# Third level's weights split over VectorE and GpSimd, and the mixed kernels one step later in a round

## The chip, the cores and the metric

The kernel runs on one core of a Trainium2 chip. The metric is the device time of one execution in microseconds (us). PE is the TensorE matmul engine, PEld its weight loads, DVE is VectorE, ACT is ScalarE, POOL is GpSimd and SP is the engine that issues most DMAs.

## The reference

Two blocks are added to a residual stream `x` of 32 x 128 x 2048 in fp32. The first block is a conditioned 1x1 convolution (a mixture of eight 128 x 128 kernels for each batch entry), followed by a dense layer of 2048 x 2048 whose weight has sixteen low-rank updates. The second is a grouped convolution of nine taps followed by a per-head feed-forward part. The change lies in the dense layer:

```python
out = jnp.einsum('bsd,od->bso', x, W) + bias
xa = jnp.einsum('bsd,erd->ebsr', x, A)
w = coeffs * scales
upd = jnp.einsum('ebsr,eor,e->bso', xa, Bf, w)
return out + upd
```

In the kernel the mixture is applied after the dense layer, so that the dense product takes `x` itself, and the low-rank updates are folded into `W`.

## The kernel before, in words

**The dense product** is a matrix product by recursion of the kind that replaces eight block products by seven (each with sums and differences of blocks as operands). The outermost level gives seven **rounds**, `ROUNDS = ("P1", "P2", "P6", "P7", "P5", "P3", "P4")`. A round has eight **steps** `g` = 0 to 7, one for each group of four batch entries. Inside a step the second level gives seven products again, named P1 to P7 too; each is four chained fp32 matmuls of 128 x 128 by 128 x 512 into a PSUM bank, which DVE then adds into an SBUF accumulator.

**The third level** is applied to one of these seven, in the rounds of `THIRD` (all but P1 and P4, with pair 3 left out in three of them). There two neighbouring steps, `g` even and `g` odd, form a **pair**. `multiply_third` runs only five of the seven products in each step (P1, P5, P6, P3, P7), and what P2 and P4 would have done for both steps is done in the odd step by seven **quarters**: each is four matmuls of 128 x 128 by 128 x 256, and their order among the products is P1, *P1q*, *P2q*, P5, *P6q*, *P5q*, P6, *P7q*, *P3q*, P3, *P4q*, P7. The operands of the quarters are
- the third level's **weights** `quarters`: sums and differences of the halves of the round's P2 weights (tile `_q0`) and P4 weights (tile `_q1`), made once in a round by `third_weights` (lines 387 to 390, in the profile `P_q`). For each of the two tiles and two values of `kc` there are four operations on 128 x 256, sixteen in all;
- the third level's **inputs** `sq`, made for each pair by `third_inputs` (lines 406 to 409): four operations on 128 x 512.

Quarters P1q and P2q read neither; P6q is the first to read both, `t[:, 1]` of each.

**The order of the work** is written out by hand: under `manual_schedule` each engine runs its instructions in program order. In step `i` of the main loop POOL first combines the next step's inputs (`x_combine`: line 282 for sums of x blocks and lines 310 to 313 for `s_P`), then makes `sq` if `g` is even (in round P6 DVE does so after the step), at `g` = 7 makes the second level's weights of the next round (`inner_weights`, lines 252 to 256, tiles `P_t`; its `t4` holds the P4 weights), and at `g` = 0 runs `third_weights`. The call `inner_weights` of step 7 comes after the `x_combine` for the next round's step 0; then follow, at `g` = 0, the `x_combine` for step 1, `sq` and `third_weights`. SP issues the loads in program order too: accumulators for the next step (`olds_load`, line 272) and x for the step after (`x_loads`, line 267). All these tiles come from one pool of 24 slots of 1 MB, and a tile waits for the release of the slot that it gets.

**Between the products** of a step `between(j)` puts small work on DVE. `mixed_kernel` builds the mixed 128 x 128 kernel of one batch entry there in eight operations (lines 533 and 535), two after each of the first four products, in steps 0 to 5 of each round from the second on; entry 15 ends with a DMA on POOL's queue (line 537). The last round P4, the convolution and the feed-forward part come after and are not touched.

Of the kernel before, what the change touches and what calls it, by code (L numbers as in the profile page):

```python
# [11 lines left out]
ALU = mybir.AluOpType  # L12
# [5 lines left out]
B = 32  # L18
L = 2048
QW = 512  # L20
KEXP = 8
# [6 lines left out]
NQ = QW // 2  # L28
# [4 lines left out]
NG = B // GB  # L33
# [17 lines left out]
THIRD = ("P2", "P6", "P7", "P5", "P3")  # L51
# [4 lines left out]
def adaln_ffn_kernel(  # L56
# [16 lines left out]
    nc = tc.nc  # L73
# [88 lines left out]
    def w_load(kh, oh, kc):  # L162
        t = slot(f"w_{kh}{oh}{kc}", (P, 2, 2, QW))
        nc.sync.dma_start(t.rearrange("p k o c -> p (k o c)"), WT[kh, oh, kc])
        return t
# [79 lines left out]
    def inner_weights(name, ts, between=lambda kc: None):  # L245

        t1, t2, t4 = (slot(f"{name}_t{k}", (P, 4, QW)) for k in (1, 2, 4))
        tt = nc.gpsimd.tensor_tensor
        for kc, t in enumerate(ts):
            between(kc)  # L250
            b11, b12, b21, b22 = (t[:, ki, oi] for ki in range(2) for oi in range(2))
            tt(t1[:, kc], b12, b11, ALU.subtract)  # L252
            tt(t2[:, kc], b22, t1[:, kc], ALU.subtract)  # L253
            tt(t4[:, kc], b21, t2[:, kc], ALU.subtract)  # L254
        for t in ts:
            tt(t[:, 0, 1], t[:, 1, 1], t[:, 0, 1], ALU.subtract)  # L256
        return {
            "P1": [t[:, 0, 0] for t in ts], "P2": [t[:, 1, 0] for t in ts],
            "P3": [t[:, 1, 1] for t in ts], "P7": [t[:, 0, 1] for t in ts],
            "P4": [t4[:, kc] for kc in range(4)], "P5": [t1[:, kc] for kc in range(4)],  # L260
            "P6": [t2[:, kc] for kc in range(4)],
        }
# [32 lines left out]
    def x_combine(r, g, ts):  # L295

        a = ts[0]
        tt = nc.gpsimd.tensor_tensor
        if r == "P6":

            b, a, c = ts
            pieces(b, b, a, ALU.add)
            pieces(a, b, c, ALU.subtract)
            part_store("s2", g, a)
        if r in ("P7", "P5", "P3"):
            pieces(a, a, ts[1], ALU.add if r == "P5" else ALU.subtract)
        xa[steps.index((r, g))] = a
        s = slot(f"s_{r}{g}", (P, 4, QW))
        a11, a12, a21, a22 = a[:, 0, 0], a[:, 1, 0], a[:, 0, 1], a[:, 1, 1]
        tt(s[:, 0], a21, a22, ALU.add)  # L310
        tt(s[:, 1], s[:, 0], a11, ALU.subtract)
        tt(s[:, 2], a11, a21, ALU.subtract)
        tt(s[:, 3], a12, s[:, 1], ALU.subtract)
        return {
            "P1": a11, "P2": a12, "P3": s[:, 3], "P4": a22,
            "P5": s[:, 0], "P6": s[:, 1], "P7": s[:, 2],
        }
# [60 lines left out]

    def third_weights(name, rhs):

        quarters, tt = [], nc.gpsimd.tensor_tensor
        for i, k in enumerate(("P2", "P4")):
            t = slot(f"{name}_q{i}", (P, 4, 2, NQ))
            q = {"P1": [], "P2": [], "P3": [], "P4": [], "P5": [], "P6": [], "P7": []}
            for kc in range(2):
                (r11, r12), (r21, r22) = (halves(rhs[k][2 * h + kc]) for h in range(2))
                tt(t[:, 0, kc], r12, r11, ALU.subtract)
                tt(t[:, 1, kc], r22, t[:, 0, kc], ALU.subtract)  # L388
                tt(t[:, 2, kc], r22, r12, ALU.subtract)
                tt(t[:, 3, kc], r21, t[:, 1, kc], ALU.subtract)  # L390
                for n, r in zip(q, (r11, r21, r22, t[:, 3, kc], t[:, 0, kc], t[:, 1, kc], t[:, 2, kc])):
                    q[n].append(r)
            quarters.append(q)
        return quarters

    def in_pair(r, g):
        return r in THIRD and (r, g // 2) not in SKIP
# [634 lines left out]
    for i, (r, g) in enumerate(steps):  # L1032
        ri = i // NG
        last_round = ri + 1 == len(ROUNDS)
        if i + 1 < len(steps):
            if i + 1 not in xs:
                xs[i + 1] = x_loads(*steps[i + 1])
            if not last_round:
                lhs[i + 1] = x_combine(*steps[i + 1], xs.pop(i + 1))
                if in_pair(r, g) and g % 2 == 0 and r != "P6":  # L1040
                    sq = third_inputs(i, nc.gpsimd)
        if i == 0:
            olds_load(0)
        if i + 1 < len(steps) and not last_round:
            olds_load(i + 1)
        ahead = i + 2 < len(steps) and ri > 0 and not last_round
        if ahead and steps[i + 2][0] != "P6":
            xs[i + 2] = x_loads(*steps[i + 2])
        if g == NG - (1 if ri else 2) and ri < len(ROUNDS) - 1:
            nxt = inner_weights(ROUNDS[ri + 1], [nxt[kc] for kc in range(4)])  # L1050
        if r in THIRD and g == 0:
            quarters = third_weights(r, rhs)

        if ri == 0:
            ks = blocks[4 + 2 * g : 6 + 2 * g]
            if ks:
                two = [wt.pop(k) for k in ks]
                w_make_two(ks, two, sa[ks[0][0]], tb[ks[0][1]])
                made.extend(ks)
                if g == 1:  # L1060
                    a_scale(1, 0, 4)
                    sa[1] = a_combine(1, nc.gpsimd.tensor_tensor)
                if g == 3:
                    part, tb[0] = b_combine(0, nc.gpsimd.tensor_tensor)
                    for _ in range(4):
                        part()
                for k, t in zip(ks, two):
                    unsummed.append((k[1], t))
                    if k[:2] == (1, 0):
                        nxt[k[2]] = t  # L1070
        elif ri + 1 < len(ROUNDS):
            for k, combine in waiting.items():
                nxt[k] = combine()
            waiting = {}
            if 2 <= g < 6:
                waiting[g - 2] = outer_weights(ROUNDS[ri + 1], g - 2)

        if last_round and g == 0:
            late_loads()
        if last_round and g == 2:  # L1080

            late["te"] = mix.rearrange("p (k r) c -> p k r c", k=2)
            nc.sync.dma_start(mix.rearrange("p k c -> p (k c)"), te_d)
        k0 = 3 * (g - NG)
        if last_round:
            stage(k0, stage_first)

        def between(j):
            b = (ri - 1) * (NG - 2) + g
            if ri > 0 and g < NG - 2 and b < B and j < KEXP // 2:  # L1090
                mixed_kernel(b, (2 * j, 2 * j + 1))
            if ri == 0 and j == 2:
                for k in blocks[6 + 2 * g : 8 + 2 * g]:
                    wt[k] = w_load(*k)
            if j == 3 and ahead and steps[i + 2][0] == "P6":
                xs[i + 2] = x_loads(*steps[i + 2])
            if ri == 0 and j in (1, 3) and unsummed:
                row_sums(*unsummed.pop())
            if ri == 0 and j == 5 and unsummed_first:
                t = unsummed_first.pop(0)  # L1100
                tt = nc.vector.tensor_tensor
                tt(wsum[:, 0, 0], wsum[:, 0, 0], t[:, 0, 0], ALU.add)
                tt(wsum[:, 0], wsum[:, 0], t[:, 1], ALU.add)
            if last_round:
                if j == 3 and i + 1 < len(steps):
                    lhs[i + 1] = x_combine(*steps[i + 1], xs.pop(i + 1))
                    olds_load(i + 1)
                if j in (2, 4):
                    stage(k0 + j // 2, stage_first)
                if j % 2:  # L1110
                    stage_third(k0 + j // 2)
                else:
                    stage(k0 + j // 2, stage_second)

        if in_pair(r, g):
            multiply_third(
                r, g, lhs.pop(i), rhs, olds.pop(i), between, quarters, sq if g % 2 else None
            )
        else:
            multiply(r, g, lhs.pop(i), rhs, olds.pop(i), between)  # L1120
        xa.pop(i - 1, None)
        if in_pair(r, g) and g % 2 == 0 and r == "P6":
            sq = third_inputs(i, nc.vector)
        next(chain, None)
        if i > 5:
            next(chain, None)
        if last_round and g >= 6:
            pair(g - 6)
        if last_round and g == 7:
            rings()  # L1130
            gather_two(0)
        if g == NG - 1 and ri + 1 < len(ROUNDS):
            rhs = nxt
            nxt = {}

    before = None
    for k, (g, h) in enumerate(heads):
# [5 lines left out]
        t = ts.pop(k)  # L1143
# [75 lines left out]
```

## Time and profile before

| | before |
|---|---|
| median of three runs | 2629.13 us (2628.73 to 2630.31) |
| the profiled execution's own time | 2628.8 us |
| its span | 2627.0 us |
| PE busy | 2591.4 us (99%) |
| DVE busy | 1449.3 us (55%) |
| POOL busy | 1356.6 us (52%) |
| granted TensorE clock, mean | 0.995 |

An engine's busy time is the sum of its instructions in the span; what is missing to the span is idle time, and the profile names for each group what ended it. A busy PE is not a PE at its peak: matmuls overlap, their ends are modelled, and a matmul at a lower granted clock counts as busy for longer. The page of the changed part covers about 300 to 1270 us of the span: rounds P2, P6, P7, P5 and P3 start their step 0 at 305.66, 493.87, 682.61, 876.42 and 1073.31 us on PE.

### The profile page before, as it was taken

The numbers are of one execution on the slowest core, as the hardware profiler recorded it, in microseconds if no ns is written. First come the engines' busy times: TensorE is split into PE (matmuls) and PEld (weight loads), VectorE is DVE, ScalarE is ACT, GpSimd is POOL, SyncE is SP. The second block draws the span as 40 slices with busy tenths as digits, with TensorE's granted clock in tenths as the row PEclk, the third lists the DMA queues.
The fourth block names the chain that finished last, engine by engine and source line by source line (L and its number), as shares of the span: only waits on it lengthen the run. The fifth ranks groups of instructions, "written<-read, shape, count | busy, mean of one in ns | idle before, by whom it ended". The sixth has DMA issues, their size and how long they took to land.

```text
span 2627.0 us, 21296 instructions
## 1 busy us (share of the span) xinstructions
PE 2591.4 (99%) x6876; PEld 1307.7 (50%) x6876; DVE 1449.3 (55%) x2290; ACT 533.2 (20%) x1099; POOL 1356.6 (52%) x1150
## 2 busy tenths in 40 slices
PE   9999999999999999999999999999999999999998
PEld 4444455455455555455444445555455544555543
DVE  5554255455344575454366666666666666666610
ACT  0000000000000000000011144444444444444432
POOL 7320667987967963976432334434443344344222
PEclk9999999999999999999999999999999999999999
DMA  8542458778456477566668798776778777787532
GB/s 318 209 166 108 172 211 330 279 280 337 187 237 258 193 294 298 208 244 236 213 217 259 215 320 284 237 228 213 245 235 250 243 224 223 236 256 229 165 121 88
DMA packets 183838, 608.27 MB, mean 232 GB/s; under 512 B 17200, under 2 KB 88368, under 8 KB 139440
## 3 DMA queue, kind: packets, MB, share of 16 engines
q1 hardware_dynamic: 149936, 473.74, 51.0%
q0 software_dynamic: 32992, 132.14, 14.9%
q10 hardware_dynamic: 800, 1.03, 0.1%
q8 instruction: 55, 0.90, 0.1%
q14 instruction: 55, 0.45, 0.1%
HBM read 372.45 MB, written 200.84 MB: 218 GB/s over the span
## 4 chain that ended last, share of the span: by engine, by line
PE 84%; POOL 9%; DMA 4%; DVE 2%; issue 1%; SPq 0%; POOLq 0%; ACT 0%; DVEq 0%; ACTq 0%
PE bank L428 17%; PE bank L807 17%; PE bank L818 16%; PE bank L348 14%; PE bank L439 7%; PE bank L663 6%; PE bank L571 4%; PE bank L223 2%; POOL xt L282 2%; DMA xt<-in_xT 1%; DMA bf_sb<-in_BfT 1%; POOL P_t L253 1%; POOL wo_P L256 1%; POOL P_t L252 1%; POOL P_t L254 1%
## 5 line engine op out<-in xcount | busy, mean ns | idle before, releaser
L807 PE MATMUL bank<-t,ws 128*128 128x512 f32 x1024 | 460.4, 592 | 0.9 <-DMA ws<-in_ffw 0.9
L818 PE MATMUL bank<-gl,ws 128*128 128x512 f32 x1024 | 460.2, 592 | 0.0
L825 POOL DMA_INDIRECT out<-t,orow x128 | 151.8, 1186 | 538.1 <-DVE t L823 467.0
L810 ACT ACTIVATE gl<-bank 128x512 f32<-128x512 f32 x512 | 306.3, 598 | 446.4 <-PE bank L807 443.3
L818 PEld LDWEIGHTS bank<-gl,ws 128*128 128x128 f32 x1024 | 194.6, 190 | 233.0 <-issue 231.5
L807 PEld LDWEIGHTS bank<-t,ws 128*128 128x128 f32 x1024 | 194.5, 190 | 227.8 <-issue 223.2
L556 POOL TENSOR_TENSOR x<-x,fb 128x512 f32<-128x512 f32 x128 | 175.4, 1399 | 213.2 <-DMA x<-in_x 151.6
L562 ACT ACTIVATE bank<-w,aggb 128x512 f32<-128x512 f32 x128 | 80.8, 684 | 918.4 <-DMA w<-w_d 901.5
L823 DVE TENSOR_TENSOR t<-bank,t 128x512 f32<-128x512 f32 x128 | 88.5, 691 | 319.4 <-PE bank L818 319.2
L428 PE MATMUL bank<-P_t,s_P 128*128 128x512 f32 x544 | 241.9, 592 | 0.0
L424 DVE TENSOR_TENSOR u<-bank,u 128x512 f32<-128x512 f32 x168 | 110.7, 687 | 193.8 <-PE bank L428 173.8
L282 POOL TENSOR_TENSOR xt<-xt,xt 128x512 f32<-128x512 f32 x128 | 159.3, 1277 | 98.4 <-DMA xt<-in_xT 96.1
L428 PE MATMUL bank<-wo_P,s_P 128*128 128x512 f32 x448 | 199.1, 592 | 0.0
L310 POOL TENSOR_TENSOR s_P<-xt 128x512 f32<-128x512 f32 x56 | 72.8, 1300 | 239.3 <-DMA xt<-in_xT 187.3
L535 DVE SCALAR_TENSOR_TENSOR ags<-mix,att_bc,ags 128x128 f32<-128x128 f32 x224 | 190.8, 852 | 4.5
L428 PEld LDWEIGHTS bank<-P_t,s_P 128*128 128x128 f32 x544 | 103.7, 191 | 115.7 <-issue 112.2
L791 POOL DMA_INDIRECT t<-hx_d,row x128 | 131.4, 1027 | 53.8 <-issue 26.0
L348 PE MATMUL bank<-P_t,s_P 128*128 128x512 f32 x352 | 154.7, 592 | 0.0
L428 PEld LDWEIGHTS bank<-wo_P,s_P 128*128 128x128 f32 x448 | 85.1, 190 | 95.2 <-issue 92.6
L663 PE MATMUL bank<-va,tw_l 128*128 128x256 f32 x512 | 122.1, 380 | 1.6 <-DVE va L647 1.5
L439 PE MATMUL bank<-P_q,sq 128*128 128x256 f32 x408 | 103.3, 401 | 17.2 <-POOL P_q L388 17.2
L663 PEld LDWEIGHTS bank<-va,tw_l 128*128 128x128 f32 x512 | 96.7, 190 | 43.8 <-issue 33.0
(191 smaller groups left out, 3560.0 us busy)
## 6 DMA issues: line engine op xcount, KB each, us to landing
xt<-in_xT SPq DMA_DIRECT2D x88, 1024.0 KB, 9.4
u<-u_d SPq DMA_DIRECT2D x40, 1024.0 KB, 8.9
wo_P<-wb_d SPq DMA_DIRECT2D x36, 1024.0 KB, 10.8
u<-c_d SPq DMA_DIRECT2D x64, 512.0 KB, 6.9
x<-in_x SPq DMA_DIRECT2D x32, 1024.0 KB, 8.1
xg<-x SPq DMA_DIRECT2D x256, 128.0 KB, 5.3
hx_d<-x1t SPq DMA_DIRECT2D x32, 1024.0 KB, 6.6
hx_d<-ht SPq DMA_DIRECT2D x32, 1024.0 KB, 7.6
```

Of the source, the lines that this page charges most:

```text
L282: nc.gpsimd.tensor_tensor(out[:, i, j], a[:, i, j], b[:, i, j], op)
L348: nc.tensor.matmul(ps, lhsT=lhs[k][:, bass.ts(kc, P)], rhs=rhs[k][kc], start=first and kc == 0, stop=last and kc == 3, skip_group_check=True,)
L428: nc.tensor.matmul(ps, lhsT=lhs[k][:, bass.ts(kc, P)], rhs=rhs[k][kc], start=first and kc == 0, stop=last and kc == 3, skip_group_check=True,)
L439: nc.tensor.matmul(out, lhsT=sq[k][:, i, bass.ts(kc, P)], rhs=quarters[i][k][kc], start=first and i == 0 and kc == 0, stop=last and i == 1 ...
L535: nc.vector.scalar_tensor_tensor(ag, mix[:, k], att, ag, ALU.mult, ALU.add)
L556: nc.gpsimd.tensor_tensor(xt[:, f], xt[:, f], late["fb"][:, f], ALU.add)
L663: nc.tensor.matmul(out, lhsT=w[:, 2 * i + r], rhs=rhs, start=first and r == 0, stop=last and r == 1, skip_group_check=True,)
L791: nc.gpsimd.indirect_dma_start(out=t.rearrange("p k t -> p (k t)"), out_offset=None, in_=hx_d[g].rearrange("l k t -> l (k t)"), in_offset= ...
L807: nc.tensor.matmul(pu, lhsT=w[:, m * P : (m + 1) * P], rhs=t[:, 0], start=True, stop=True)
L810: nc.scalar.activation(gl[m], pu, AF.Gelu)
L818: nc.tensor.matmul(pd, lhsT=w[:, (MC + m) * P : (MC + m + 1) * P], rhs=gl[m], start=(m == 0), stop=(m == MC - 1),)
L825: nc.gpsimd.indirect_dma_start(out=out, out_offset=bass.IndirectOffsetOnAxis(ap=orow[:, g, h : h + 1], axis=0), in_=t[:, 1], in_offset=None,)
```

## The change

`third_weights` keeps its eight POOL operations for P2's tile `_q0`, each on 128 x 256. P4's tile `_q1` is filled by four operations of 128 x 512 (both `kc` at once, read from `t4`), which are handed back as a list and issued on DVE, one in each of `between(0)` to `between(3)` of step 0. The call moves up: it now stands behind step 0's `x_combine` and ahead of `third_inputs`, and so also ahead of `olds_load` and the `x_loads` of that step in the order in which slots are taken. The mixed kernels move by one step in every round but the last: from steps 0 to 5 to steps 1 to 6.

```diff
@@ inner_weights
         return {
+            "t4": t4,
@@ third_weights
-        quarters, tt = [], nc.gpsimd.tensor_tensor
+
+        ops, quarters = [], []
         for i, k in enumerate(("P2", "P4")):
             t = slot(f"{name}_q{i}", (P, 4, 2, NQ))
             q = {"P1": [], "P2": [], "P3": [], "P4": [], "P5": [], "P6": [], "P7": []}
             for kc in range(2):
                 (r11, r12), (r21, r22) = (halves(rhs[k][2 * h + kc]) for h in range(2))
-                tt(t[:, 0, kc], r12, r11, ALU.subtract)
-                tt(t[:, 1, kc], r22, t[:, 0, kc], ALU.subtract)
-                tt(t[:, 2, kc], r22, r12, ALU.subtract)
-                tt(t[:, 3, kc], r21, t[:, 1, kc], ALU.subtract)
                 for n, r in zip(q, (r11, r21, r22, t[:, 3, kc], t[:, 0, kc], t[:, 1, kc], t[:, 2, kc])):
                     q[n].append(r)
+                if i == 0:
+                    tt = nc.gpsimd.tensor_tensor
+                    tt(t[:, 0, kc], r12, r11, ALU.subtract)
+                    tt(t[:, 1, kc], r22, t[:, 0, kc], ALU.subtract)
+                    tt(t[:, 2, kc], r22, r12, ALU.subtract)
+                    tt(t[:, 3, kc], r21, t[:, 1, kc], ALU.subtract)
             quarters.append(q)
-        return quarters
+        (r11, r12), (r21, r22) = (
+            [rhs["t4"][:, 2 * h : 2 * h + 2, n * NQ : (n + 1) * NQ] for n in range(2)]
+            for h in range(2)
+        )
+        ops = [
+            (t[:, 0], r12, r11), (t[:, 1], r22, t[:, 0]), (t[:, 2], r22, r12), (t[:, 3], r21, t[:, 1])
+        ]
+        return quarters, ops
@@ main loop
                 lhs[i + 1] = x_combine(*steps[i + 1], xs.pop(i + 1))
+                if r in THIRD and g == 0:
+                    quarters, quarter_ops = third_weights(r, rhs)
                 if in_pair(r, g) and g % 2 == 0 and r != "P6":
                     sq = third_inputs(i, nc.gpsimd)
...
-        if r in THIRD and g == 0:
-            quarters = third_weights(r, rhs)
@@ between(j)
-            b = (ri - 1) * (NG - 2) + g
-            if ri > 0 and g < NG - 2 and b < B and j < KEXP // 2:
+
+            g0 = g - (not last_round)
+            b = (ri - 1) * (NG - 2) + g0
+            if ri > 0 and 0 <= g0 < NG - 2 and b < B and j < KEXP // 2:
                 mixed_kernel(b, (2 * j, 2 * j + 1))
...
+            if r in THIRD and j < 4 and quarter_ops:
+                nc.vector.tensor_tensor(*quarter_ops.pop(0), ALU.subtract)
```

## The prediction

> **What bounds the kernel now.** The page comes first, then the waits of PE, the timeline of PE and POOL where PE waits, and stretches of that place.
>
> ```profile
> PE 2591.4 (99%) x6876; PEld 1307.7 (50%) x6876; DVE 1449.3 (55%) x2290; ACT 533.2 (20%) x1099; POOL 1356.6 (52%) x1150
> L439 PE MATMUL bank<-P_q,sq 128*128 128x256 f32 x408 | 103.3, 401 | 17.2 <-POOL P_q L388 17.2
> ```
>
> PE fills the span: 2627.0 - 2591.4 = 35.6 us idle is all that a better order can win on the face of it. The second row says who owns most: quarters that wait for the third level's weights. The waits of PE (total, times, longest) agree:
>
> ```profile
> PE bank L439 <- POOL P_q L388: 17.2, 12, 2.2
> PE bank L223 <- DVE w L226: 3.1, 3, 2.3
> ```
>
> All twelve fall in the first odd step of the five rounds. In round P5, PE's timeline (start, length, engine, line, count, wait) shows:
>
> ```profile
> 900.47 3.60 PE L428 MATMUL bank<-P_t,s_P 128*128 128x512 f32 x8
> 904.43 0.70 PE L439 MATMUL bank<-P_q,sq 128*128 128x256 f32 x2 [0.36 <-POOL P_q L388]
> 907.33 0.70 PE L439 MATMUL bank<-P_q,sq 128*128 128x256 f32 x2 [2.20 <-POOL P_q L388]
> 910.17 1.22 PE L439 MATMUL bank<-P_q,sq 128*128 128x256 f32 x2 [2.14 <-POOL P_q L388]
> 913.01 4.08 PE L439 MATMUL bank<-P_q,sq 128*128 128x256 f32 x10 [1.62 <-POOL P_q L388]
> 916.93 0.59 PE L428 MATMUL bank<-P_t,s_P 128*128 128x512 f32 x1
> ```
>
> The same two quarters (P6q, P5q) take 3.45 us undisturbed: 857.49 to 860.94 in the pair before. Here they could start at 900.47 + 3.43 = 903.90, and product P6 follows at 916.93, so the **loss** is 13.03 - 3.45 = 9.58 us, more than the 6.3 us of waits. The stretches (length, PE busy, ..., clock) say why:
>
> ```profile
> 857.49:860.94 3.45, 3.45 (x17) 3.04 (x16) 1.38 (x2) 0.00 (x0) 3.29 (x3) 1.00 0.35 95
> 913.00:916.93 3.93, 3.92 (x11) 3.22 (x11) 1.29 (x2) 0.00 (x0) 3.93 (x5) 0.57 0.00 0
> ```
>
> After the waits the granted clock is 0.57, and ten short records take 4.08 us. Read in the same way, from the start of P6q to product P6 less 3.45: P2 333.14 to 337.48, 0.89; P6 521.35 to 526.22, 1.42; P7 710.09 to 721.52, 7.98; P3 1100.80 to 1111.41, 7.16. **The sum is 27.0 us**, and that is the prize. POOL in the same place:
>
> ```profile
> 896.54 1.26 POOL L313 TENSOR_TENSOR s_P<-xt,s_P 128x512 f32<-128x512 f32 x1
> 897.76 1.27 POOL L406 TENSOR_TENSOR sq<-xt 128x512 f32<-128x512 f32 x1
> ...
> 902.84 0.73 POOL L387 TENSOR_TENSOR P_q<-wo_P 128x256 f32<-128x256 f32 x1
> ...
> 912.23 0.72 POOL L388 TENSOR_TENSOR P_q<-P_t,P_q 128x256 f32<-128x256 f32 x1
> ```
>
> POOL has no gap here. After the step's `x_combine` (end 897.76) come `sq` (5.08 us) and sixteen operations of about 0.72 us; the fourteenth ends at 912.95 and releases the last half of P6q at 913.01.
>
> **What the Trainium skill says.** TensorE: Matmul & The Clock Gate, "Why this matters for your kernels", asks for "No PE-idle gaps >~3µs between matmul bursts", else the clock drops to half. The trace agrees in substance: 0.57 after several waits of about 2 us that leave PE mostly idle, 1.00 in the undisturbed pair. SBUF — State Buffer, "SBUF: two separate sides", says that a VectorE operation with two SBUF inputs and a GpSimd operation that reads SBUF exclude each other for a whole instruction. The trace agrees: where DVE makes `sq` in round P6 (513.34 to 516.7), POOL's `P_q` operations take 1.05 to 1.18 us in place of 0.72.
>
> **The change part by part.**
>
> *P4's quarters leave POOL.* Eight operations go, 8 x 0.72 = 5.8 us in each round; P6q no longer waits for the second tile's chain on POOL.
>
> *P2's quarters go ahead of `sq`.* From the end of `x_combine` POOL now runs eight `P_q` operations (in P5 902.84 to 908.59, 5.75 us) and two of `sq` (897.76 to 900.33 for lines 406 and 407, 2.6 us), and P6q may start: 8.4 us after `x_combine`, where it was 15.2 us. P5q needs only the first `sq` operation; P7q and P3q, which need the third and fourth, come 6.9 us and more after P6q. P2's weights are raw blocks, so the call being earlier waits for nothing.
>
> *P4's quarters on DVE.* Four of 128 x 512 in step 0. The same shape on DVE takes 0.68 (line 958) to 0.86 us (lines 406 to 409 beside POOL); waiting out a POOL operation of 1.27 us, at most about 2. Each stands behind an add of 0.69 us, or two in P5 (1.29), in a product of 3.43 us, so adds are not late for PE: 0. They are ready by step 0 + 16 us, and P6q comes at + 27.5. The wait that is added is on `t4`: its last piece is made at 882.5 in P5 (line 254), while the second DVE operation, the first that needs it, cannot start before about 883.8; elsewhere `t4` is older. Queued behind that wait are adds with over 1 us of slack: 0.
>
> *What those four cost POOL.* They exclude POOL operations ahead of `x_combine`'s end. In P6 four DVE operations stretched four of POOL by 0.33 to 0.45, some 1.7 us in all; the mixed kernels that they replace cost POOL about 0.3 (5.14 in place of 4.94 for four of line 282, and the like). Net 1.4 us; bounds -0.3 (all fall into gaps) and 2.4 (0.68 each).
>
> *Mixed kernels from step 0 to step 6.* Eight operations, 8 x 0.85 = 6.8 us of DVE, beside 24 us of products whose adds take at most 9 (round P5, two accumulators). Step 0 of P5 carries the same load now, with DVE up to two products behind and no wait on PE: 0, at worst 1 us. The DMA of entry 15 on POOL's queue (now issued at 780.25 after 13.89 us of waiting for DVE) moves to step 4 of P7 and holds POOL to about 800; behind it is the `x_combine` for step 6, 10 us long, needed at 830.00: 20 us of slack.
>
> *Slots and SP.* Two tiles are taken earlier, so `sq`, the accumulators and the x loads of step 0 get slots two places later. SP issues no more DMAs than before, and the longest wait that this shows on SP for a slot held by POOL is 25.0 us. Accumulators land about 8 to 10 us before their first add (P7: issued about 686.5, 8.9 us to land, needed at 703.4); x for step 2 lands some 20 us before POOL takes it up. I take 0, because almost all slots in question are weights of the round before, released by then.
>
> **The sum.** P6q starts at the end of `x_combine` + 1.4 + 8.4 + 0.1 (from release to matmul). P7: 701.80 + 9.9 = 711.7 against 710.09, a stall of 1.6. P5: 897.76 + 9.9 = 907.7 against 903.90, 3.8. P3: 1092.11 + 9.9 = 1102.0 against 1100.80, 1.2. P2 and P6: none (in P6 `x_combine` ends at 512.03, the tile's sixth operation by about 519.5, `sq` at 516.7, against 521.35). That leaves 6.6, and 0.7 for a chance of a lowered clock after P5's one gap (0 to 2): 7.3 us. The gain is 27.0 - 7.3 = 19.7 us, on the profiled execution 2628.8 - 19.7 = 2609.1; the median stood 0.3 above it, so 2609.4. With POOL delayed by -0.3 the stalls shrink to 2.2 and the gain is 24.8; with 2.4 and the clock lowered once they are 11.6 and the gain is 15.4. Everything after is led by PE, so a gain here arrives whole at the end. This case: 2604 to 2614.
>
> **The rivals.** *All of it goes*, 2602 to 2604: POOL, relieved of 5.8 us a round, comes earlier to the next round's `x_combine`. For P7 that can be (POOL waits there on x loads that its own releases start). Against it stands P5: its `inner_weights` wait for PE (line 252 0.94 us, line 253 2.25 us), so they move with PE and P5's 2 us stay.
>
> *Half of it*, 2614 to 2624: the exclusion costs POOL more than four times 0.45, since DVE's operations come at full length against operations of 1.27 us, or the clock drops in all three rounds: 3 x 2 us of slow matmuls on top of 9 us of stalls gives 2617.
>
> *It does not do what it says*, 2624 to 2631: the first DVE operation on `_q1` meets a slot still held, and P6q waits for DVE as long as it did for POOL. Slack is 27.5 - 16 = 11 us, so this takes a hold that no view hints at.
>
> *Slower*: the accumulators for step 1 fall on slots that are released only within step 0, and DVE's adds in step 1 and with them PE wait for loads. A slip below about 8 us costs nothing, each us above it costs 1 us in each of five rounds; past 8 + 5 = 13 us the gain of 19.7 is gone and 5.3 more lost, with 2636 as a fair value. The x tile of `x_combine` in step 0, released at 696.7, is the one such slot in P7; it gives 10 us, and more likely to an x load.
>
> **How the numbers follow.** A measurement of this kernel tells about 0.2% (5.3 us) from no change. Chances: forecast 0.66, all of it 0.10, half 0.12, no effect 0.06, slower 0.06. Faster is 0.66 + 0.10 + 0.12 = 0.88, within 0.2% 0.06, slower 0.06. The range 2602 to 2617 holds the first two and the nearer part of the third.
>
> **What would show it.** Right: no wait of PE on `P_q` in P2 and P6; single gaps of about 1.6, 3.8 and 1.2 us in P7, P5 and P3, released by `sq` line 407, not by line 388; the clock at 1.00 after them or nearly; PE busy down by some 10 us and idle by some 10; four DVE operations of 0.7 to 1.3 us in each first step. Wrong: PE waiting in step 1 for adds, a load of line 272 landing after its add was due, a gap at step 6 behind the mixed kernels, or `x_combine` of step 1 ending more than 22 us after step 0's start.

## The result and the profile after

The changed kernel took 2622.64 us (median of eight runs, 2620.45 to 2625.94), the kernel before 2628.93 us (eight runs). The ratio is 0.9977 [0.9967, 0.9988], so 6.3 us were gained. The forecast was 2609.4 us with a range from 2602 to 2617: the sign was right, the size was not, and the result lies above the range. The profiled execution took 2625.11 us with a span of 2623.0.

The waits of PE in the kernel after (total, times, longest) show the first half of the forecast come true and a new first place:

```profile
PE bank L450 <- DVE u L458: 9.8, 1, 9.8
PE bank L450 <- POOL sq L418: 6.6, 3, 3.5
```

`P_q` is gone from the list. The three waits of the second row are the three forecast ones, released by `sq` (line 418 now). They are 2.27 us long in round P7, 3.51 in P5 and 0.87 in P3. The first row is a single wait for DVE. Sections 1 and 5 of the page after:

```profile
PE 2590.8 (99%) x6876; PEld 1310.3 (50%) x6876; DVE 1459.2 (56%) x2310; ACT 532.9 (20%) x1099; POOL 1337.5 (51%) x1110
...
L450 PE MATMUL bank<-P_q,sq 128*128 128x256 f32 x408 | 101.3, 401 | 16.4 <-DVE u L458 9.8
```

The quarters' row stood at 17.2 us idle before, all for POOL. It still stands at 16.4, but most of it now waits for DVE. PE's busy time hardly fell (2591.4 us before): the kernel after still has groups of matmuls at a lowered clock, which count as busy for longer. Three of its four places on the PE timeline (start, length, engine, line, count, wait):

```profile
710.65 5.41 PE L450 MATMUL bank<-P_q,sq 128*128 128x256 f32 x16 [2.27 <-POOL sq L418]
815.23 6.66 PE L450 MATMUL bank<-P_q,sq 128*128 128x256 f32 x16 [9.78 <-DVE u L458]
...
914.78 6.39 PE L450 MATMUL bank<-P_q,sq 128*128 128x256 f32 x16 [3.51 <-POOL sq L418]
```

At full clock such a group takes 3.72 us (it does so in other kernels below), so these groups lost 1.7, 2.9 and 2.7 us after their gaps. The second place is not in step 1 but in **step 5 of round P7**. Its stretch (length, PE busy, ..., clock) stands below that of a quiet place in the same step:

```profile
801.00:804.43 3.43, 3.43 (x12) 1.89 (x11) 0.00 (x0) 0.00 (x0) 3.43 (x4) 1.00 1.03 423
815.23:821.90 6.67, 6.67 (x17) 5.40 (x18) 2.55 (x5) 0.00 (x0) 0.00 (x0) 0.55 0.06 22
```

Read as in the prediction (from the time at which P6q could start to product P6, less 3.45), this one place loses 13.0 us. The DVE timeline says what DVE did meanwhile:

```profile
798.65 0.69 DVE L435 TENSOR_TENSOR u<-bank,u 128x512 f32<-128x512 f32 x1 [2.20 <-issue]
813.81 0.29 DVE L544 TENSOR_SCALAR ags<-mix,att_bc 128x128 f32<-128x128 f32 x1 [14.46 <-POOL xt L283]
814.13 0.35 DVE L546 SCALAR_TENSOR_TENSOR ags<-mix,att_bc,ags 128x128 f32<-128x128 f32 x1
814.40 1.48 DVE L458 TENSOR_TENSOR u<-bank,u 128x512 f32<-128x512 f32 x2
```

DVE stood still for 14.46 us ahead of line 544, the first operation of a mixed kernel. What ended that wait is POOL's work on an x tile, which this operation does not read. It waits for a **slot**: entry 16 is the first of the second half of the batch, and for it `mixed_kernel` takes a new tile `ags_16` out of the pool. In the program as built, that tile has the address of the second x block for step 7, which in turn has the address of the first half's `ags_0`. POOL's timeline shows that chain (line 548 stores `ags_0`, line 283 at 808.85 uses up the x block):

```profile
793.37 0.56 POOL L548 DMA_DIRECT2D ag_d<-ags  x1 [12.54 <-DVE ags L546]
...
808.85 4.92 POOL L283 TENSOR_TENSOR xt<-xt,xt 128x512 f32<-128x512 f32 x4
```

The store of line 548 took 6.2 us from 793.37 to land, and SP issued the second of the two x loads at 799.7. That load had landed by 806.9 at the latest; POOL, busy without a gap from 793.95 on, took the block up at 808.85. It was done at 813.77, and DVE went on at 813.81. Behind DVE's operation stood the add of line 458 that PE waited for. Before the change, entry 16 came in step 4, and its slot was the one that the accumulator of step 3 (`u`) had just left. The row then read:

```profile
790.17 0.81 DVE L533 TENSOR_SCALAR ags<-mix,att_bc 128x128 f32<-128x128 f32 x1 [2.21 <-DMA u_d<-u]
```

That wait of 2.21 us was on view before the prediction and was not read there.

### The profile page after: what moved, and what is told of

Same layout as the page of the kernel before. It is cut to its first block, busy times and chain, and to the rows that moved or that the text cites. A ratio compares the mean times of both kernels' runs of the same rounds, so it can differ in the third digit from the quotient of the medians.

```text
span 2623.0 us, 21287 instructions
## 1 busy us (share of the span) xinstructions
PE 2590.8 (99%) x6876; PEld 1310.3 (50%) x6876; DVE 1459.2 (56%) x2310; ACT 532.9 (20%) x1099; POOL 1337.5 (51%) x1110
## 4 chain that ended last, share of the span: by engine, by line
PE 78%; POOL 13%; DMA 5%; issue 2%; DVE 1%; SPq 0%; POOLq 0%; ACT 0%; DVEq 0%; ACTq 0%
PE bank L818 17%; PE bank L829 16%; PE bank L349 15%; PE bank L439 13%; PE bank L674 6%; PE bank L450 5%; POOL xt L283 5%; PE bank L582 4%; PE bank L223 2%; DMA xt<-in_xT 2%; POOL wo_P L283 1%; POOL wo_P L256 1%; DMA bf_sb<-in_BfT 1%; POOL P_t L253 1%; POOL s_P L311 1%
## 5 line engine op out<-in xcount | busy, mean ns | idle before, releaser
L546 DVE SCALAR_TENSOR_TENSOR ags<-mix,att_bc,ags 128x128 f32<-128x128 f32 x224 | 177.1, 791 | 4.5
L450 PE MATMUL bank<-P_q,sq 128*128 128x256 f32 x408 | 101.3, 401 | 16.4 <-DVE u L458 9.8
```

The source lines that it names most:

```text
L450: nc.tensor.matmul(out, lhsT=sq[k][:, i, bass.ts(kc, P)], rhs=quarters[i][k][kc], start=first and i == 0 and kc == 0, stop=last and i == 1 ...
L546: nc.vector.scalar_tensor_tensor(ag, mix[:, k], att, ag, ALU.mult, ALU.add)
```

## The experiments

Each kernel was run in alternation with the kernel before, whose medians lay between 2629.1 and 2629.5 us. "Losses" are always those of the prediction's reading. The diffs are against the changed kernel unless another is named.

**1. Mixed kernels back in steps 0 to 5.**

```diff
-            g0 = g - (not last_round)
+            g0 = g
```

> The changed kernel with the mixed kernels put back to steps 0 to 5; the quarters stay as changed. Theory S (one slot: DVE's first operation of mixed kernel 16 takes a slot that POOL releases late, and PE loses 13.0 us behind it in round P7): the tile is again taken in step 4, on a slot that a store has long left, so the 13.0 us are gone; steps 0 carry both works on DVE, which may cost POOL 0.3 to 1 us a round. 2629 - 6.3 - 13 + 2 = 2612 us (2608 to 2615), no wait of PE on DVE. Theory L (load: DVE is simply busier, wherever the work stands): DVE is busiest now in the steps where POOL is latest, so the stalls in P7, P5 and P3 grow by several us and the time stays at 2620 to 2626.

Measured: 2609.59 us, 0.9929 [0.9916, 0.9943]. The stall in step 5 is gone. The first odd steps lose 0.7 (P6), 2.1 (P7), 1.8 (P5) and 1.1 us (P3), all at full clock. PE's waits in this kernel:

```profile
PE bank L450 <- POOL sq L418: 4.1, 3, 1.8
...
PE bank L439 <- DVE u L435: 1.8, 1, 1.8
```

The second row lies in step 0 of P5, where DVE now has the mixed kernel and P4's quarters together, works without a gap, and comes 1.8 us late with its adds. So the other two parts of the change bring 20 us without the move, and the move's own advantage (no such wait in step 0) is small.

**2. The move alone**, on the kernel before: the same line `g0 = g - (not last_round)`, its condition, and nothing else.

> The kernel before with only the mixed kernels moved one step. Theory S: the same wait of DVE in step 5 of round P7 (about 14 us) and of PE (about 10 us, 13 us with the lowered clock), on top of the 27.0 us of before: 2629 + 13 = 2642 us (2638 to 2645). Theory L: the first steps lose DVE's interference, so 2626 to 2629 us and no such wait.

Measured: 2641.43 us, 1.0044 [1.0030, 1.0058]. The move costs 12 us by itself, with the same signature in the waits of PE:

```profile
PE bank L439 <- POOL P_q L388: 16.6, 10, 2.2
PE bank L439 <- DVE u L447: 9.8, 1, 9.8
```

**3. The slot taken one step earlier.** Everything is as in the changed kernel, but the first of entry 16's eight operations, the one that takes the slot, is issued at the end of step 4.

```diff
-                mixed_kernel(b, (2 * j, 2 * j + 1))
+                mixed_kernel(b, (2 * j, 2 * j + 1)[b == NCH and j == 0 :])
+            if r == "P7" and g == 4 and j == 4:
+                mixed_kernel(NCH, (0,))
```

> The changed kernel, with the first of the eight operations of mixed kernel 16 (the one that takes the slot) moved from between(0) of step 5 to between(4) of step 4 in round P7; POOL is still held by the DMA of entry 15. Theory S: the slot comes from an accumulator stored long before, DVE does not wait, PE's 13.0 us are gone: 2623 - 13 = 2610 us (2607 to 2613). Theory H (POOL's hold of 12.5 us by that DMA is what counts, and x_combine is late behind it): POOL is as late as before and PE waits on it or on DVE in step 5 again: 2620 to 2625 us.

Measured: 2610.59 us, 0.9930 [0.9916, 0.9943]. In the program as built the tile again has the slot of step 3's accumulator, and DVE does not wait for it:

```profile
793.58 1.29 DVE L435 TENSOR_TENSOR u<-bank,u 128x512 f32<-128x512 f32 x2 [2.10 <-PE bank L439]
794.78 2.60 DVE L544 TENSOR_SCALAR ags<-mix,att_bc 128x128 f32<-128x128 f32 x1
```

(The operation's 2.60 us, where it took 0.29 above, end as POOL's sums of line 283 do, at about 797.3.) POOL is held here as well, and it is done with the x of step 7 at 817.5, later than in the changed kernel:

```profile
791.78 0.56 POOL L548 DMA_DIRECT2D ag_d<-ags  x1 [12.57 <-DVE ags L546]
...
812.51 4.95 POOL L283 TENSOR_TENSOR xt<-xt,xt 128x512 f32<-128x512 f32 x4 [5.07 <-DMA xt<-in_xT]
```

One operation of 128 x 128, issued earlier, gives back 12 us. DVE does the same work and POOL is no earlier, so it was the slot, and neither the amount of DVE's work nor POOL's lateness by itself.

**4. POOL freed of the store.** The rival explanation put the stall down to POOL, held for 12.54 us by line 548. Here ACT issues that DMA.

```diff
-            nc.gpsimd.dma_start(ag_d[b // NCH], ...)
+            nc.scalar.dma_start(ag_d[b // NCH], ...)
```

> The changed kernel with the DMA of the mixed kernels' tile issued by ACT in place of POOL, so that POOL isn't held for 12.5 us in step 4 of round P7; tile 16 takes the same slot as in the changed kernel, behind the same x tile. Theory S: POOL reaches that x tile up to 12.5 us earlier if its load has landed, DVE's wait of 14.5 us shrinks to 2 to 8 us, PE's to 0 to 3: 2610 to 2617 us. Theory H: the same, and all of the loss goes: 2610 us. If the time stays at 2620 or more, the x tile was late for another reason, its load.

Measured: 2621.52 us, 0.9970 [0.9958, 0.9982], which neither theory's range holds; it is the third case that the expectation names, a load that is late. POOL is no longer held by the store, yet it is held all the same, and DVE waits almost as long (POOL's timeline, then DVE's):

```profile
792.10 5.04 POOL L283 TENSOR_TENSOR xt<-xt,xt 128x512 f32<-128x512 f32 x4 [11.10 <-DMA xt<-in_xT]
...
807.52 4.92 POOL L283 TENSOR_TENSOR xt<-xt,xt 128x512 f32<-128x512 f32 x4 [0.36 <-DMA xt<-in_xT]
```

```profile
812.48 0.29 DVE L544 TENSOR_SCALAR ags<-mix,att_bc 128x128 f32<-128x128 f32 x1 [12.96 <-POOL xt L283]
```

Now POOL waits for the x of step 6 (11.10 us). ACT issued the store at 794.82 and it took 6.0 us to land; SP issued the second x load for step 7 at 800.9, and POOL, which waited for it, took it up at 807.52. POOL's hold is worth 1.5 us of DVE's wait and 2.5 of the loss (10.5 in place of 13.0). What stays is a chain through one slot: the last operation on `ags_0`, its store, the x load, POOL's sums, then `ags_16`. In the changed kernel the last link was POOL's backlog, here it is the load.

**5. P4's quarters on DVE, old order on POOL** (on experiment 1): `third_weights` is called behind `third_inputs` and the loads, where it was.

> Theory S (slot theory): the mixed kernels stay in steps 0 to 5, so there is no stall behind a mixed kernel. Of the other two parts only the move of P4's quarters to VectorE is kept; on POOL the order stays x's quarters first, then P2's eight. P6q's last operand is then ready 1.4 + 5.08 + 6 x 0.72 = 10.8 us after x_combine, where both parts together need 9.8 to 9.9. That alone is 1 us more in each of P7, P5 and P3 than e1_no_shift, plus lowered clock [...](up to 2.8 in each): 2609.6 + 3 + 4 = 2617 (2611 to 2622). Rival O (the order does the work): without the reorder POOL is still the last in each round and the time stays near the changed kernel or above, 2621 to 2627.

Measured: 2614.16 us, 0.9947 [0.9934, 0.9961]: 15 of the 20 us come from moving P4's quarters. Losses rise from experiment 1's values to 4.7 in P7 (of which 1.7 is a slow group), 2.4 in P5 and 1.9 in P3.

**6. The order alone** (on experiment 1): P4's eight operations of 128 x 256 stay on POOL behind `sq`, P2's eight go ahead of it (part of the diff).

```diff
...
+                    for op in quarter_ops:
+                        nc.gpsimd.tensor_tensor(*op, ALU.subtract)
+                    quarter_ops = []
```

> All sixteen quarter operations stay on POOL, P2's ahead of x's quarters and P4's behind them; the mixed kernels stay in steps 0 to 5. Theory S: POOL has the same 5.75 + 5.08 + 6 x 0.72 = 15.1 us to do between x_combine and P6q's last operand as in the kernel before (15.2), so the order by itself brings nothing: losses near 27 us and 2629 (2625 to 2631). Rival O: the order alone brings several us, because P2's weights no longer stand behind x's quarters: 2615 to 2623.

Measured: 2628.59 us, 1.0001 [0.9992, 1.0009]. The order is worth nothing here, where the last operand still stands behind the same sum of POOL operations. With P4's on DVE it is worth the 4.6 us between experiments 5 and 1.

**7. P2's quarters on DVE as well** (on experiment 3): two of them are issued ahead of each of P4's four (part of the diff).

```diff
...
-                nc.vector.tensor_tensor(*quarter_ops.pop(0), ALU.subtract)
+                for op in quarter_ops.pop(0):
+                    nc.vector.tensor_tensor(*op, ALU.subtract)
```

> e4_ags_early with P2's eight quarter operations on VectorE too, two beside each of P4's four, so that POOL has only x's quarters behind x_combine. Theory S (POOL's count between x_combine and P6q sets what is left): POOL needs 2.6 us of sq instead of 8.4, and loses perhaps 3 us more in x_combine to VectorE's eight operations, so P6q's operand comes 3 us earlier than in e4_ags_early; its losses of 2.8 in P7, 5.5 in P5 and 0.6 in P3 shrink to 0, 1 and 0: 2603 (2601 to 2606). Rival V (VectorE becomes the bound): eight more operations in step 0 put the adds behind by more than their slack, above all in P5 with two accumulators, and PE waits for VectorE 1 to 3 us in each round: 2610 to 2620. Rival X (exclusion): POOL's x_combine is stretched by what it is relieved of, and the time is that of e4_ags_early, 2608 to 2612.

Measured: 2625.03 us, 0.9984 [0.9977, 0.9991]. PE waits here neither for `P_q` nor for `sq` from POOL, but for DVE's adds (waits of PE):

```profile
PE bank L438 <- DVE u L434: 9.5, 3, 7.2
PE bank L449 <- DVE p L457: 4.4, 1, 4.4
...
PE bank L449 <- DVE u L457: 3.6, 1, 3.6
```

The longest of them, 7.2 us in step 0 of P7, is no matter of DVE's load. DVE stood still there:

```profile
700.42 0.42 DVE L1111 TENSOR_TENSOR P_q<-wo_P 128x256 f32<-128x256 f32 x1 [9.18 <-POOL xt L283]
```

This operation reads no x tile either. In the program as built its tile `_q0` of round P7 has the slot of an x block for step 1, which POOL's sums of line 283 use up to 700.4: a slot again, and it cost PE 9.9 us with the slow matmuls behind it. The waits in P6 and P5 are of the kind of rival V: DVE runs there with hardly a gap and its adds come late. They cost more than V's 1 to 3 us in these two rounds, and nothing in P2 and P3. Less the 9.9 us the time would be about 2615 us (an estimate), inside V's range. The DVE timeline of step 0 in round P6 gives the price of one operation:

```profile
506.37 0.89 DVE L1111 TENSOR_TENSOR P_q<-wo_P 128x256 f32<-128x256 f32 x1
507.29 0.43 DVE L1111 TENSOR_TENSOR P_q<-wo_P,P_q 128x256 f32<-128x256 f32 x1
507.63 2.05 DVE L1111 TENSOR_TENSOR P_q<-P_t 128x512 f32<-128x512 f32 x1
...
511.02 1.48 DVE L1111 TENSOR_TENSOR P_q<-wo_P,P_q 128x256 f32<-128x256 f32 x1
```

The operation at 507.29 ran while POOL only issued a DMA (507.27 to 507.83): 0.43 us. Its equal at 511.02, beside POOL's sums of 128 x 512, took 1.48. DVE's busy time rose from experiment 3 by 1512.6 - 1462.0 = 51 us for 40 operations, 1.3 us each. At that price P4's four fit into step 0 on DVE, and P2's eight beside them do not in P6 and P5.

**8. The gap filled in part** (on experiment 3): in the first pair of P5, quarter P2q is done twice, four matmuls more.

```diff
+        if r == "P5" and g == 1:
+            quarter("P2", qz, True, True)
```

> e4_ags_early with quarter P2q of round P5's first pair done twice (four matmuls more, about 1.7 us of PE, same values), so that PE's gap ahead of P6q there shrinks from about 3.5 to 1.8 us with no other engine touched. Theory C (the slow matmuls behind the gap come from the gap's own length): the matmuls behind it run at full clock, the ten records after P6q's start take 3.7 instead of 6.4 us, product P6 starts 2 to 3 us earlier in spite of the added work; 2608 (2605 to 2611), read from the place and not from the total. Theory N (the gap has nothing to do with the clock there): the same ten records still take about 6.4 us, and the time is that of e4_ags_early, 2610.6.

Measured: 2608.24 us, 0.9920 [0.9907, 0.9934], an interval that overlaps that of experiment 3. The totals do not tell them apart, so the place decides. PE's timeline in experiment 3, then here:

```profile
900.21 5.41 PE L450 MATMUL bank<-P_q,sq 128*128 128x256 f32 x16 [3.51 <-POOL sq L418]
```

```profile
713.17 5.41 PE L450 MATMUL bank<-P_q,sq 128*128 128x256 f32 x16 [3.01 <-POOL sq L418]
...
904.34 3.72 PE L450 MATMUL bank<-P_q,sq 128*128 128x256 f32 x16 [1.81 <-POOL sq L418]
```

In P5 (second row) the wait fell from 3.51 to 1.81 us and the same sixteen matmuls from 5.41 to 3.72. Theory C holds in this pair of executions: the gap of 3.51 us cost 1.7 us more than itself. In P7 (first row), where nothing was edited, this execution had a longer wait than experiment 3 and paid the 1.7 there. Experiment 3 had:

```profile
710.75 3.72 PE L450 MATMUL bank<-P_q,sq 128*128 128x256 f32 x16 [2.56 <-POOL sq L418]
```

**9. and 10. The operand needed later.** On experiment 3 and on experiment 1: in the first odd step of each round, P6q and P5q come behind product P6.

```diff
+        late_q = int(sq is not None and g == 1)
+        for part in range(2):
+            if part == late_q:
                 quarter("P6", qx if sq else None, False, False, (0, 1))
                 quarter("P5", qy if sq else None, True, False, (1, 1))
+            else:
                 product("P6", px, False, False)
                 add(0, 1, px)
         between(2)
```

> e4_ags_early, and in the first odd step of each round the quarters P6q and P5q come behind product P6 and its add, not ahead of them; nothing else moves. No engine gets less to do. Theory S (what is left are PE's waits for POOL's sq and the lowered clock behind them): the operand is due one product, 3.43 us, later, so the gaps of 2.6, 3.5 and 0.9 us in P7, P5 and P3 become 0, about 0.1 and 0, no slow matmuls follow, and the 8.9 us of losses become about 0.5: 2602 (2600 to 2605). Rival W (VectorE's adds): with P5, P6 and two quarters back to back their adds bunch, P7q must wait until VectorE has read P6q's bank, and PE waits for VectorE up to 1 us in each of five rounds, 2604 to 2609. Rival K (the time left over is lost elsewhere, later in POOL's chain, when PE comes earlier): the time stays at 2608 to 2612.

> The same reordering of the quarters on e1_no_shift, so with the mixed kernels back in steps 0 to 5. Theory S: its losses of 5.7 us go, PE's wait of 1.8 us for VectorE in the first step of P5 stays: 2604 (2602 to 2607), 1 to 2 us above e10_late_p6q. Rival W: PE waits for VectorE in the first odd steps too, more than in e10_late_p6q since the mixed kernels' operations stand nearer: 2607 to 2612. Rival K: 2608 to 2612.

Measured: 2601.38 us, 0.9895 [0.9878, 0.9911], and 2602.35 us, 0.9897 [0.9881, 0.9914]. These are the fastest of all, ahead of both the kernel before and the changed one. The 1 us between the two is within their spread. The PE timeline of experiment 9 in P5, where 9.6 us were lost before:

```profile
891.42 7.03 PE L439 MATMUL bank<-P_t,s_P 128*128 128x512 f32 x16
898.55 5.45 PE L450 MATMUL bank<-P_q,sq 128*128 128x256 f32 x24
903.83 1.03 PE L450 MATMUL bank<-wo_P,sq 128*128 128x256 f32 x4
```

Products P5 and P6 run into the quarters with a tenth of a microsecond between them. No wait of PE on line 439 or 450 is left in experiment 9, and in experiment 10 only the 1.8 us in step 0 of P5 that theory S had kept, so rivals W and K fell.

All kernels fit one sum: the span less the losses read at the named places, each from one profiled execution.

| kernel | span | losses in the first odd steps | other waits, with what followed | span less both |
|---|---|---|---|---|
| before | 2627.0 | 27.0 | | 2600.0 |
| after | 2623.0 | 11.8 | 13.0 (slot) | 2598.2 |
| 1 | 2605.9 | 5.7 | 1.8 (DVE) | 2598.4 |
| 2 | 2640.7 | 26.6 | 11.8 (slot) | 2602.3 |
| 3 | 2608.5 | 8.9 | | 2599.6 |
| 4 | 2619.3 | 10.5 | 10.5 (slot) | 2598.3 |
| 5 | 2611.7 | 9.9 | 1.8 (DVE) | 2600.0 |
| 6 | 2627.0 | 26.8 | | 2600.2 |
| 7 | 2624.1 | 11.9 | 12.3 (slot 9.9, DVE 2.3) | 2599.9 |
| 8 | 2608.6 | 7.7 | 1.7 (added quarter) | 2599.2 |
| 9 | 2599.7 | 0.3 | | 2599.4 |
| 10 | 2598.9 | 0.0 | 1.8 (DVE) | 2597.1 |

(For 7, the 12.3 are waits in step 0: in P7 7.2 for the slot and 2.75 of slow matmuls behind it, in P5 2.3 for DVE.)

The last column stays within 2597 to 2602, although the spans differ by 42 us: these places account for nearly all of what the kernels differ in.

## Why the prediction was wrong, point by point

**The prize, 27.0 us: right.** Experiment 9 took 27.3 us off the span by removing those losses.

**P4's quarters leave POOL; P2's go ahead: right, and together.** Without the move (experiment 1) the kernel took 2609.59 us, where the forecast for the whole change was 2609.4. That agreement is in part luck, with offsetting parts: stalls of 2.1, 1.8 and 1.1 us in P7, P5 and P3 against 1.6, 3.8 and 1.2, plus 0.7 in P6 and 1.8 of waiting for DVE, which were put at none.

**"Slots and SP ... I take 0": this step failed.** It went through `sq`, the accumulators and the x loads, and left out a tile that the change itself moves: `ags_16`. With it fell the "0, at worst 1 us" for the mixed kernels' move, which counted DVE's operations and not what the first of them must wait for. The real price was 13.0 us in the profiled execution, by experiments 1 to 3 12 to 13 in the medians. The slack of 20 us given for entry 15's DMA was also argued from POOL alone: the DMA's end is what frees `ags_0`'s slot, and on it hung the x load and then `ags_16`. The rival named *slower* had the right kind of mechanism, an add behind a slot that is released late, but the wrong tile and place, and it counted on five rounds where there was one. The sign "a gap at step 6 behind the mixed kernels" came near: the gap stood at step 5. The measured time lies in the range of the rival *half of it* (2614 to 2624), but not for its reasons: of the 17.5 us lost beyond the forecast, 13.0 come from the slot.

**"0.7 for a chance of a lowered clock (0 to 2)": too small.** The profiled execution paid 1.7 us in P7 and 2.7 in P5 (6.39 for a group of 3.72), 4.4 in all. In P7 the prediction gave no such cost.

**The stalls themselves: nearly right.** The loss in P5 was 6.45 us, less 2.7 for the clock 3.7, against 3.8. The loss in P3 was 1.15 against 1.2. The loss in P7 was 4.2, less 1.7 for the clock 2.5, against 1.6: PE could start P6q 1.9 us earlier than before, and the operand came only 1.1 us earlier than forecast. The exclusion term of 1.4 us was good: in P7 the four operations of line 256 and the four of line 283 took 5.83 us each where they had taken 4.99 and 5.14, 1.5 us more. The price of DVE's own four was read too low in one place: 0.86 us for lines 406 to 409 is a mean over three pairs, and in the pair that ran beside POOL they took 0.87 to 1.21. P4's four took 0.68 to 1.80 us, still under the "at most about 2".

**The sum again.** Forecast losses were 7.3. Measured were 11.8 in the first odd steps, 4.5 more, 3.7 of it clock, and 13.0 in step 5: 24.8. The span fell by 4.0 rather than by 2.2, and waits of PE outside the changed part were shorter in this execution (on line 223 3.1 before, 1.2 after). The median of the eight runs is 2.5 us below the profiled execution. Which of the losses the other runs escaped is not known, since only the profiled one left a trace; a clock lowered for less time fits, for their mean granted clock was 0.995 to 0.997 against its 0.994.

## What to carry to other kernels

When a step that takes a tile out of a shared pool is moved, ask which tile had its slot last and who must finish before it is free: the wait then sits on an engine that has nothing to do with that tile, and everything queued behind it waits too. It happened twice here, to `ags_16` and in experiment 7 to `_q0`. Count the whole work of an engine up to the operand that is needed last, since reordering did nothing here while that sum stayed, and price work that is moved to another engine at its duration there, beside its neighbour. And before taking more work away from a late engine, look whether the waiting one can do something else first: one product moved ahead of two quarters brought 7 to 9 us more.

## What the runs showed of the hardware that was not expected

A single short gap was enough for the lowered clock, and its length alone did not decide. After single waits of up to 1.81 us (experiments 1 and 8) the sixteen matmuls took 3.72 us; after 3.01 us (experiment 8 in P7) and 3.51 us (experiment 3 in P5) they took 5.41. Between them both occurred: 2.27 us in P7 of the changed kernel gave 5.41, 2.56 us in P7 of experiment 3 gave 3.72. "No PE-idle gaps >~3µs" in the Trainium skill (TensorE: Matmul & The Clock Gate, "Why this matters for your kernels") is thus about right here, but one wait of 2.27 us was enough once.

The exclusion of DVE and POOL was priced in the prediction by what POOL loses, 0.33 to 0.45 us. Experiment 7 shows that DVE loses more on a short operation: 1.48 us for one that takes 0.43 alone. The 1.05 us between them come near the 1.27 us of one of POOL's operations, as if DVE waited one out; no run here isolates this.
